# An expert list after the first half of a batch pair, and a routing moved ahead of left-over rounds

## The chip, the cores and the metric

The kernel runs on one core of one Trainium2 chip. The metric is the device time of one execution in microseconds; the median of three runs is shown. Five engines with queues of their own work side by side: PE (matrix multiplication, results go to PSUM), DVE (vector operations), ACT (activation functions and copies), POOL (here mainly indirect DMAs) and SP (DMA issues). Each takes its instructions in the order in which they were written into its queue and waits at the head of the queue for what the instruction needs.

## The reference

Four layers, each added to a running x of 4 sequences of 1024 tokens of width 256, in float32, each behind a layer norm:

```python
# layer 1: gated recurrence over the 1024 tokens, 64 states
m_new = max(m + lf, li); c = exp(m + lf - m_new) * c + exp(li - m_new) * z
x = x + (o * tanh(c)) @ Wp.T + bp
# layer 2: mixture of 8 experts (hidden width 512), the best 2 of each token
p, e = softmax(top_2(xn @ gate.T)); h1, h2 = split(xn @ w12[e].T)
x = x + sum_k p_k * (silu(h1) * h2) @ w3[e].T
# layer 3: causal attention, 16 heads of width 64
# layer 4: mixture of 32 experts (hidden width 128) with the best 4 of each
# token, at most 256 places an expert, and a shared expert beside it
x = x + sum_k w_k * expert[e_k](xn) + shared(xn)
```

## The kernel before

**Order of the work.** Most of the program is written in plain order and a planner sets the order of each engine's queue from it: an instruction that stands earlier in the program goes first when both could run by the planner's own clock, and a later one may fill a gap. Attention's steps (`run_steps`) and PE's part of the first experts (`l2_experts`) are fixed in the order written. The queues are fixed before the program starts[...].

**Layers 1 and 2.** The tokens are cut into four units: unit u is one half (512 tokens) of each of two sequences. `l1_unit(u)` is the recurrence of a unit, `l2_route(u)` its routing. Routing computes the gate scores (L396), takes the best two of eight (L407 to L412), counts how many tokens of each expert stand before each token (L424 to L427), and turns that into a place in a queue of that expert in HBM (`slots`, `row`, L429 to L435). Then POOL writes the rows of x into the queues, 16 indirect DMAs a unit (`scatter`, L245). Each new scatter waits for the eighth before it.

The experts work on tiles of 128 rows of one queue. Which tiles there are is known only at run time, so DVE builds a list on the chip: the lengths of the queues (`l2_lengths`), the whole or part tiles in them (`l2_count`), their running sum (`l2_cum`), an offset for each expert (`l2_shift`), and for each tile its expert and its first row (`l2_tiles`). There are three lists. List A is made after unit 1: 25 tiles (`NQ_A`), the number of whole tiles that 4096 entries in eight queues have at least. Lists B and C are made after unit 3 and hold the rest. `done` says how many tiles of each expert list A has taken. `l2_back` computes for each token in which of the output tiles its two results will lie; for that it adds to the token's place an offset that depends on which list the tile came from, with one bound between each two lists.

`l2_experts` runs over the tiles in the order of the lists. `l2_load` (L578) reads the first row from the list on SP and loads 128 rows; it waits for the last eight scatters of the units that the list covers (`nsent1` scatters for list A, all for B and C). It runs four tiles ahead. A tile is scaled on DVE (L586), transposed (L591), multiplied with the expert's w12 (L608), put through Silu on ACT (L613) and a product on DVE (L614), transposed again (L620, L622), multiplied with w3 (L628), copied (L632) and stored by SP (L633). Until tile 12 the two PSUM results of a tile share one bank; from tile 12 (`T_LATE`), when the recurrence's PSUM banks are free, the output has two banks of its own. The first 68 tiles always run, and three more under a condition.

**Layers 3 and 4.** Attention runs over four sequences, eight pairs of heads each. Beside attention of sequence b+1 runs layer 4's routing of sequence b (`l4_route`, two halves of 512 tokens). Beside the last sequence runs `l4_experts_beside`: twelve expert tiles of the first three sequences, in rounds of two tiles. A round has a load of rows of `xs_d` into `room` on SP and of weights into `w_pairs` on POOL (both in `l4_load`, L1105 and L1110), transposes (`pta`), two matmul steps (`pea`, `pya`), and two indirect DMAs that write the results to `yt_d`. These pieces are a list of jobs (`Beside`), of which attention's steps call a piece here and there. What is left when attention ends is worked off afterwards:

```python
drain(l3_out(B - 1, ps_s, "s"))
while beside.jobs or beside.job is not None:
    beside.step()
late = []
for h in range(2):
    drain(l4_route(B - 1, h, sm, ps_s, "s", late))
```

`l3_out` is attention's output projection (`pz`). All PSUM tiles of these lines come from one pool of seven banks, `ps_s`. `Scatters` is the writer of the routed rows (`to_slots`, into `xs_d`) and of the expert outputs (`to_tokens`, into `yt_d`); its `wait` makes a load wait for the latest eight writes that were issued before it in the program. `l4_route` of the last sequence writes only the first of the four choices at once (eight scatters, L857); the rest stand under a condition.

**The tail.** Behind that come the count of places over the last sequence (`pn`, L1758), the list of its four expert tiles (`l4_list_b`) and a flag on DVE, 24 takes of finished expert outputs of the first three sequences (`l4_take`, L1727, 6.1 MB on SP, which wait for the last eight writes to `yt_d`), a branch on the flag (L1837, L1841), the four expert tiles (`l4_get` and so on, whose row loads wait for the routing's scatters), the adds of all takes (`l4_add`, L1734), eight more takes and the stores of the result.

Of the kernel before, what the change touches and what calls it, by code (L numbers as in the profile page):

```python
# [33 lines left out]


NQ_A = -(-(B * S - E0 * (P - 1)) // P)
NQ_1 = (B * S + E0 * (P - 1)) // P
NQT = (B * S * K0 + E0 * (P - 1)) // P
NQ_S = B * S * K0 // P + E0 // 2
# [17 lines left out]
def block_kernel(  # L57
# [119 lines left out]
    with ExitStack() as ph:  # L177
# [280 lines left out]
        def l2_lengths(u, name):  # L458

            pn = ps_t.tile([P, E0], F32, name=f"pn_{name}", tag="t")  # L460
            nc.tensor.matmul(pn, ones, runs[u][:, NU, :], start=True, stop=True)
            return pn

        def l2_count(pn, op, name):

            n = 2 * NU + 1 if op == ALU.is_le else 4 * NU
            first = 1 if op == ALU.is_le else 0
            more = sm.tile([P, D + 2], F32, name=f"more_{name}", tag="xn", bufs=4)
            more = more[:, : E0 * (n - first)].rearrange("p (e n) -> p e n", e=E0)
            nc.vector.tensor_tensor(  # L470
                more, whole[:, first:n].unsqueeze(1).to_broadcast([P, E0, n - first]),
                pn.unsqueeze(2).to_broadcast([P, E0, n - first]), op,
            )
            cnt = rt.tile([P, E0], F32, name=f"cnt_{name}")
            nc.vector.tensor_reduce(cnt, more, AX.X, ALU.add)
            return cnt

        def l2_cum(cnt, name):
            n = cnt.shape[-1]
            cum = rt.tile([P, n], F32, name=f"cum_{name}")  # L480
            nc.vector.tensor_tensor_scan(cum, ones[:, :n], cnt, 0.0, ALU.mult, ALU.add)
            return cum

        def l2_shift(cum, cnt, start, base, name):

            sh = rt.tile([P, E0], F32, name=f"shift_{name}")
            nc.vector.tensor_sub(sh, cum, cnt)
            if start is not None:
                nc.vector.tensor_sub(sh, sh, start)
            nc.vector.tensor_scalar(sh, sh, float(P), float(P * base), ALU.mult, ALU.add)  # L490
            return sh

        def l2_tiles(cum, shifts, base, skip, n, name):


            ns = len(shifts)
            past = rt.tile([P, n, ns * E0], F32, name=f"past_{name}", tag="past")
            nc.vector.tensor_tensor(
                past, tile_no[:, skip : skip + n].unsqueeze(2).to_broadcast([P, n, ns * E0]),
                cum.unsqueeze(1).to_broadcast([P, n, ns * E0]), ALU.is_ge,  # L500
            )

            val = rt.tile([P, 2, ns * E0 + 1], F32, name=f"val_{name}")
            for s, sh in enumerate(shifts):
                es = slice(s * E0, (s + 1) * E0)
                nc.vector.tensor_copy(val[:, 0, es], expert_no)
                nc.vector.tensor_sub(val[:, 1, es], base1, sh)
            nc.vector.memset(val[:, 0, ns * E0 :], 0.0)
            nc.vector.memset(val[:, 1, ns * E0 :], float(E0 * QROWS + 1))
            step = rt.tile([P, 2, ns * E0], F32, name=f"step_{name}")  # L510
            nc.vector.tensor_sub(step, val[:, :, 1:], val[:, :, : ns * E0])
            out_i = []
            for w in range(2):
                prod = rt.tile([P, n, ns * E0], F32, name=f"prod_{name}_{w}", tag="prod")
                nc.vector.tensor_mul(
                    prod, past, step[:, w, :].unsqueeze(1).to_broadcast([P, n, ns * E0])
                )
                f = rt.tile([P, n], F32, name=f"desc_{name}_{w}")
                nc.vector.tensor_reduce(f, prod, AX.X, ALU.add)
                i = rt.tile([P, n], I32, name=f"desc_i_{name}_{w}")  # L520
                if w == 0:
                    nc.vector.tensor_copy(i, f)
                else:

                    off = rt.tile([P, n], F32, name=f"off_{name}")
                    nc.vector.tensor_scalar(
                        off, past[:, :, ns * E0 - 1], -1.0, float(-P), ALU.add, ALU.mult
                    )
                    pos = rt.tile([P, n], F32, name=f"tile_pos_{name}")
                    nc.vector.tensor_scalar(pos, tile_no[:, skip : skip + n], float(base), None, ALU.add)  # L530
                    nc.vector.tensor_mul(off, off, pos)
                    nc.vector.tensor_add(f, f, off)
                    nc.vector.tensor_scalar(
                        i, f, val[:, 1, 0:1], -1.0, ALU.add, ALU.add
                    )
                out_i.append(i)
            return out_i


        def l2_back(ts, n, shifts, bounds, name):  # L540
            r = sm.tile([P, n, E0], F32, name=f"back_{name}", tag="back", bufs=1)

            def wide(t):
                return t.unsqueeze(1).to_broadcast([P, n, E0])

            first = rt.tile([P, E0], F32, name=f"first_{name}")
            nc.vector.tensor_sub(first, shifts[0], base1)
            nc.vector.tensor_add(r, slots[:, ts, :], wide(first))
            for j, bound in enumerate(bounds):
                lim = rt.tile([P, E0], F32, name=f"lim_{name}_{j}")  # L550
                nc.vector.scalar_tensor_tensor(lim, bound, float(P), base1, ALU.mult, ALU.add)
                dif = rt.tile([P, E0], F32, name=f"dif_{name}_{j}")
                nc.vector.tensor_sub(dif, shifts[j + 1], shifts[j])
                ge = sm.tile([P, n, E0], F32, name=f"ge_{name}_{j}", tag="ge", bufs=1)
                nc.vector.tensor_tensor(ge, slots[:, ts, :], wide(lim), ALU.is_ge)
                nc.vector.tensor_mul(ge, ge, wide(dif))
                nc.vector.tensor_add(r, r, ge)
            back = rt.tile([P, K0, n], F32, name=f"backf_{name}")
            for k in range(K0):
                g = sm.tile([P, n, E0], F32, name=f"bk_{name}_{k}", tag="ge", bufs=1)  # L560
                nc.vector.tensor_tensor(
                    g, slots[:, ts, :], chosen[:, k, ts].unsqueeze(2).to_broadcast([P, n, E0]),
                    ALU.is_equal,
                )
                nc.vector.tensor_mul(g, g, r)
                nc.vector.tensor_reduce(back[:, k, :], g, AX.X, ALU.add)
            back_i = keep0.tile([P, K0, n], I32, name=f"back_{name}")
            nc.vector.tensor_copy(back_i, back)
            return back_i
# [129 lines left out]
        def in_sequence(u):  # L699
            return [(v, n) for par in range(2) for v in (u, u + 1) for n in range(par * HT0, par * HT0 + HT0)]  # L700


        for u in range(2):
            l1_unit(u)
            l2_route(u)
        nsent1 = len(sent)
        pn1 = l2_lengths(1, "half")
        fullA = l2_count(pn1, ALU.is_le, "whole")
        cnt1 = l2_count(pn1, ALU.is_lt, "half")
        cumA = l2_cum(fullA, "whole")  # L710
        shA = l2_shift(cumA, fullA, None, 0, "A")
        listed = [l2_tiles(cumA, [shA], 0, 0, NQ_A, "A")]

        done = rt.tile([P, E0], F32, name="done")
        nc.vector.tensor_sub(done, fullA, cumA)
        nc.vector.tensor_scalar(done, done, float(NQ_A), 0.0, ALU.add, ALU.max)
        nc.vector.tensor_tensor(done, done, fullA, ALU.min)
        seg = rt.tile([P, 2 * E0], F32, name="seg")
        nc.vector.tensor_sub(seg[:, :E0], cnt1, done)
        cumB1 = l2_cum(seg[:, :E0], "B1")  # L720
        shB1 = l2_shift(cumB1, seg[:, :E0], done, NQ_A, "B1")
        back1 = l2_back(slice(0, 2 * NU), 2 * NU, [shA, shB1], [done], "1")


        for u in (2, 3):
# [17 lines left out]
        half = (NQT - NQ_A) // 2  # L743
        listed.append(l2_tiles(cumB, [shB1, shB2], NQ_A, 0, half, "B"))
        listed.append(l2_tiles(cumB, [shB1, shB2], NQ_A, half, NQT - NQ_A - half, "C"))
        back2 = l2_back(slice(2 * NU, 4 * NU), 2 * NU, [shA, shB1, shB2], [done, cnt1], "2")

        first = in_sequence(0)
        adds = {}
# [1 line left out]
        def behind(t):  # L751
# [8 lines left out]

        tiles = [
            (exp_i[0:1, j : j + 1], src_i[0:1, j : j + 1], n)
            for (exp_i, src_i), n in zip(listed, (nsent1, len(sent), len(sent)))
            for j in range(exp_i.shape[-1])
        ]
        with tc.manual_schedule(engines={mybir.EngineType.PE}):
# [492 lines left out]
    def drain(pieces):  # L1259
        for _ in pieces:  # L1260
            pass
# [4 lines left out]
    with ExitStack() as ph:  # L1266
# [430 lines left out]
        with tc.manual_schedule():  # L1697
            run_steps()
        drain(l3_out(B - 1, ps_s, "s"))
        while beside.jobs or beside.job is not None:  # L1700
            beside.step()
        late = []
        for h in range(2):
            drain(l4_route(B - 1, h, sm, ps_s, "s", late))

    taken.close()

# [220 lines left out]
```

## Time and profile before

| what | us |
|---|---|
| median of three runs (2060.64 to 2064.38) | 2062.74 |
| the profiled execution, its own time | 2178.17 |
| its span, first to last instruction | 2176.5 |
| PE busy in it (86%) | 1881.8 |
| DVE busy (58%) | 1258.6 |
| ACT busy (44%) | 959.4 |
| first scatter of units 0, 1, 2, 3 (POOL) | 65.3, 115.2, 178.8, 233.3 |
| first transpose of an expert tile (PE) | 141.2 |
| last matmul of the 68 expert tiles begins | 625.6 |
| attention's output projection ends | about 2074 |

The mean granted clock of PE in the profiled execution is 0.928 of full speed. A line of the page's slices has one digit for each of 40 equal parts of the span (54.4 us each): the busy share of an engine in tenths, or the granted clock in tenths. A line of a timeline has the start in us, the duration in us, the engine, the line of the program, the operation, what it writes and reads, how many instructions were merged, and in brackets how long the engine stood idle before and what ended that. A line of windows has for each stretch the busy time and the number of instructions of PE, PE's weight loads, DVE, ACT and POOL.

### The profile page before, as it was taken

The page shows a single profiled execution, that of the slowest core. Times are in us where ns is not written, and L with a number is a line of the kernel's source. Part 1 is how long each engine was busy: PE and PEld are TensorE (multiplying, and loading weights), DVE is VectorE, ACT ScalarE, POOL GpSimd, SP SyncE. Part 2 cuts the span into 40 slices and gives each one's busy share as a digit, 9 for nine tenths or more (in the row PEclk, how much of TensorE's full clock was granted, in tenths as well). Part 3 has the DMA queues.
Part 4 walks back from the last instruction along what each step waited for, and adds up shares of the span by engine and source line. Part 5 has one row for each costly group of instructions (what it writes and reads, how often), then busy time and mean ns, then how long its engine had stood idle before and what let it go on. Part 6 is the DMA issues. An engine that isn't in the chain of part 4 may idle for free.

```text
span 2176.5 us, 45180 instructions
## 1 busy us (share of the span) xinstructions
PE 1881.8 (86%) x17612; PEld 1223.1 (56%) x17612; DVE 1258.6 (58%) x4101; ACT 959.4 (44%) x2485; POOL 272.3 (13%) x307
## 2 busy tenths in 40 slices
PE   5668799999999999999988979997988997978863
PEld 3434456665656666666555656564655664646642
DVE  5676422234237777656756654774766475757556
ACT  3244222222236666645555543554545363645310
POOL 0333400022003200000020110002020002020121
PEclk7678799999999999999998989998999998989986
DMA  8112211122135433000000000000000000001135
GB/s 328 39 62 68 77 42 48 46 72 77 56 93 165 147 104 116 20 2 2 2 16 6 2 2 1 2 2 1 2 2 2 2 2 2 2 2 57 49 109 183
DMA packets 87151, 109.23 MB, mean 50 GB/s; under 512 B 13838, under 2 KB 76650, under 8 KB 85776
## 3 DMA queue, kind: packets, MB, share of 16 engines
q1 hardware_dynamic: 66528, 73.41, 10.2%
q0 software_dynamic: 15168, 27.05, 4.1%
q10 hardware_dynamic: 5232, 5.78, 0.8%
q8 instruction: 143, 2.34, 0.5%
q14 instruction: 80, 0.66, 0.1%
HBM read 51.75 MB, written 64.77 MB: 54 GB/s over the span
## 4 chain that ended last, share of the span: by engine, by line
PE 49%; DVE 11%; ACT 3%; issue 3%; another core or an unknown queue 3%; DMA 2%; SPq 0%; DVEq 0%; POOL 0%; ACTq 0%; POOLq 0%
PE ps L1450 10%; PE pa L1536 8%; PE pt L1500 7%; PE pq L901 6%; PE pz L901 5%; PE pk L901 5%; PE pv L901 5%; DVE ps L1466 3%; ACT pe L1479 2%; DMA xs_d<-x,row_l 1%; DVE pT L1521 1%; PE s_l L901 1%; DVE nm L1464 1%; PE sy L901 1%
## 5 line engine op out<-in xcount | busy, mean ns | idle before, releaser
L1479 ACT ACTIVATE pe<-ps,nm 128x512 f32<-128x512 f32 (+3 forms) x768 | 439.5, 578 | 279.7 <-DVE nm L1466 268.1
L1536 PE MATMUL pa<-pT,v 128*64 128x128 f32 (+1 forms) x4096 | 326.8, 291 | 3.5 <-issue 3.5
L1500 PE MATMUL pt<-ident,pe 64*128 64x64 f32 x4608 | 251.6, 231 | 90.4 <-ACT pT L1521 34.5
L1500 PEld LDWEIGHTS pt<-ident,pe 64*128 64x128 f32 x4608 | 211.6, 141 | 183.0 <-issue 79.2
L1450 PE MATMUL ps<-k,q 64*128 64x512 f32 (+3 forms) x1536 | 308.1, 509 | 5.5 <-issue 5.5
L1536 PEld LDWEIGHTS pa<-pT,v 128*64 128x64 f32 x4096 | 243.5, 138 | 106.6 <-issue 88.9
L1464 DVE TENSOR_REDUCE nm<-ps 128x1 f32<-128x512 f32 x256 | 175.9, 687 | 147.3 <-PE ps L1450 121.6
L608 PE MATMUL ph<-w_t,xgT 128*128 x544 | 259.2, 618 | 0.7
L1521 ACT COPY pT<-pt 128x512 f32<-128x512 f32 (+2 forms) x384 | 179.4, 520 | 172.6 <-PE pt L1500 163.0
L857 POOL DMA_INDIRECT xs_d<-x,row_l x104 | 102.7, 988 | 1117.6 <-DVE second L1009 1065.4
L1450 PEld LDWEIGHTS ps<-k,q 64*128 64x128 f32 x1536 | 137.7, 191 | 79.7 <-issue 66.9
L1521 DVE COPY pT<-pt 128x256 f32<-128x256 f32 (+3 forms) x384 | 178.5, 506 | 1.8 <-remote 1.5
L1466 DVE CUSTOM_DVE_ANT_0 ps<-ps,mask_a,nm 128x128 f32<-128x128 f32 (+3 forms) x256 | 143.2, 559 | 42.2 <-DVE nm L1464 9.9
L608 PEld LDWEIGHTS ph<-w_t,xgT 128*128 128x128 f32 x544 | 100.9, 197 | 104.5 <-issue 104.4
L1479 ACT ACTIVATION_READ_ACCUMULATOR pe<-ps,nm 128x1 f32 x768 | 152.1, 198 | 0.0
L901 PE MATMUL pq<-l_xT,w_pairs 128*64 128x512 f32 x448 | 110.8, 616 | 29.7 <-ACT pe L1479 28.5
L1466 DVE CUSTOM_DVE_ANT_0 ps<-ps,mask_a 128x128 f32<-128x128 f32 (+3 forms) x256 | 119.7, 518 | 23.5 <-PE ps L1450 21.8
L901 PE MATMUL pz<-wo_t,y 128*64 128x256 f32 x1024 | 115.0, 379 | 0.0
L901 PE MATMUL pv<-w_pairs,l_xT 128*64 128x128 f32 x1792 | 111.3, 278 | 2.9 <-ACT pe L1479 2.9
L628 PE MATMUL py<-w_t,hidT 128*128 x464 | 109.6, 379 | 0.0
L901 PE MATMUL pk<-l_xT,w_pairs 128*64 128x512 f32 x448 | 107.2, 599 | 1.1 <-ACT pe L1479 1.1
L901 PEld LDWEIGHTS pv<-w_pairs,l_xT 128*64 128x64 f32 x1792 | 100.4, 139 | 5.7 <-ACT pe L1479 3.6
(411 smaller groups left out, 2216.0 us busy)
## 6 DMA issues: line engine op xcount, KB each, us to landing
yt_d<-zeros SPq DMA_DIRECT2D x32, 512.0 KB
xg<-xe_d SPq DMA_DIRECT2D x68, 129.0 KB
yq_d<-ys SPq DMA_DIRECT2D x68, 128.0 KB
xs_d<-zeros SPq DMA_DIRECT2D x65, 131.5 KB
w_t<-w_dram SPq DMA_DIRECT2D x8, 1024.0 KB
w_pairs<-e_w_dram POOLq DMA_DIRECT2D x12, 384.0 KB
x<-x_in_dram SPq DMA_DIRECT2D x8, 512.0 KB
w_t<-w_dram SPq DMA_DIRECT2D x8, 512.0 KB
```

Of the source, the lines that this page charges most:

```text
L608: nc.tensor.matmul(pt, xgT[:, c, :], w[:, c, k * H0 : (k + 1) * H0], start=(c == 0), stop=(c == NC_ - 1),)
L628: nc.tensor.matmul(py, hidT[:, c, :], w[:, c, :], start=(c == 0), stop=(c == H0 // P - 1))
L857: i = nc.gpsimd.indirect_dma_start(out=self.out, out_offset=bass.IndirectOffsetOnAxis(ap=idx, axis=0), in_=src, in_offset=None, bounds_che ...
L901: nc.tensor.matmul(out[r], lhsT[:, r], rhs, start=start, stop=stop)
L1450: nc.tensor.matmul(t[:, :n], qs[b, p][rows, i * P : (i + 1) * P], ks[b, p][rows, kc * 512 : kc * 512 + n], start=True, stop=True,)
L1464: nc.vector.tensor_reduce(m[:, 0:1], t, AX.X, ALU.min)
L1466: nc.vector.tensor_tensor_reduce(out=t[:, :n], in0=t[:, :n], in1=mask[:, 512 - n :], scale=1.0, scalar=-LOWEST if kc == 0 else m[:, 0:1], ...
L1479: inst = nc.scalar.activation(pe[:, :n], sps.pop((u, k, par))[:, :n], AF.Exp, bias=ms[u, i, par][:, 1:2], scale=-1.0, accum_out=ls[b, p][: ...
L1500: nc.tensor.transpose(pts[u][r][:, j, par, :], pes[u, k, par][rows, j * P : (j + 1) * P], ident[rows, rows],)
L1521: copy(to, pts[u][r][:, :n])
L1536: nc.tensor.matmul(pas[0][rows, cols], vs[b, p][:, j, rows], pTs[u][:, j, par, a * P :], start=(j == 0), stop=(j == nb - 1),)
```

## The change

In front, unit 0's routing is followed by a list of its own: nine tiles (`NQ_A0`), the number of whole tiles that 2048 entries in eight queues have at least. Their loads wait only for unit 0's scatters. List A after unit 1 then holds the other 16 of the 25, starting behind what the first list has taken; the small helper `l2_listed` computes what a list has taken of each expert, and both calls of `l2_back` get one more offset and one more bound. The number of tiles and their work stay the same. In the tail, the routing of the last sequence is moved in front of the loop that works off the left-over rounds.

```diff
+NQ_A0 = -(-(B * S // 2 - E0 * (P - 1)) // P)
...
-        for u in range(2):
-            l1_unit(u)
-            l2_route(u)
+        def l2_listed(cum, seg, n, name):
+
+            t = rt.tile([P, E0], F32, name=f"among_{name}")
+            nc.vector.tensor_sub(t, seg, cum)
+            nc.vector.tensor_scalar(t, t, float(n), 0.0, ALU.add, ALU.max)
+            nc.vector.tensor_tensor(t, t, seg, ALU.min)
+            return t
+
+
+        l1_unit(0)
+        l2_route(0)
+        nsent0 = len(sent)
+        full0 = l2_count(l2_lengths(0, "unit"), ALU.is_le, "whole0")
+        cum0 = l2_cum(full0, "whole0")
+        sh0 = l2_shift(cum0, full0, None, 0, "A0")
+        listed = [l2_tiles(cum0, [sh0], 0, 0, NQ_A0, "A0")]
+        done0 = l2_listed(cum0, full0, NQ_A0, "A0")
+
+
+        l1_unit(1)
+        l2_route(1)
         nsent1 = len(sent)
         pn1 = l2_lengths(1, "half")
         fullA = l2_count(pn1, ALU.is_le, "whole")
         cnt1 = l2_count(pn1, ALU.is_lt, "half")
-        cumA = l2_cum(fullA, "whole")
-        shA = l2_shift(cumA, fullA, None, 0, "A")
-        listed = [l2_tiles(cumA, [shA], 0, 0, NQ_A, "A")]
-
-        done = rt.tile([P, E0], F32, name="done")
-        nc.vector.tensor_sub(done, fullA, cumA)
-        nc.vector.tensor_scalar(done, done, float(NQ_A), 0.0, ALU.add, ALU.max)
-        nc.vector.tensor_tensor(done, done, fullA, ALU.min)
+        segA = rt.tile([P, E0], F32, name="segA")
+        nc.vector.tensor_sub(segA, fullA, done0)
+        cumA = l2_cum(segA, "whole")
+        shA = l2_shift(cumA, segA, done0, NQ_A0, "A")
+        listed.append(l2_tiles(cumA, [shA], NQ_A0, 0, NQ_A - NQ_A0, "A"))
+        done = l2_listed(cumA, segA, NQ_A - NQ_A0, "A")
+        nc.vector.tensor_add(done, done, done0)
...
-        back1 = l2_back(slice(0, 2 * NU), 2 * NU, [shA, shB1], [done], "1")
+        back1 = l2_back(slice(0, 2 * NU), 2 * NU, [sh0, shA, shB1], [done0, done], "1")
...
-        back2 = l2_back(slice(2 * NU, 4 * NU), 2 * NU, [shA, shB1, shB2], [done, cnt1], "2")
+        back2 = l2_back(slice(2 * NU, 4 * NU), 2 * NU, [sh0, shA, shB1, shB2], [done0, done, cnt1], "2")
...
-            for (exp_i, src_i), n in zip(listed, (nsent1, len(sent), len(sent)))
+            for (exp_i, src_i), n in zip(listed, (nsent0, nsent1, len(sent), len(sent)))
...
         drain(l3_out(B - 1, ps_s, "s"))
-        while beside.jobs or beside.job is not None:
-            beside.step()
         late = []
         for h in range(2):
             drain(l4_route(B - 1, h, sm, ps_s, "s", late))
+        while beside.jobs or beside.job is not None:
+            beside.step()
```

## The prediction

> **What bounds the kernel now.** I read the slices of the span first, then the windows of the first 350 us, then the timelines of each engine at both ends. The slices, then three windows (PE, PEld, DVE, ACT and POOL busy in us, clock, DMA share, GB/s):
>
> ```profile
> PE   5668799999999999999988979997988997978863
> PEclk7678799999999999999998989998999998989986
> 75.00:100.00 25.00, 11.57 (x43) 6.67 (x40) 17.57 (x51) 8.89 (x13) 9.63 (x9) 0.65 0.15 53
> 100.00:125.00 25.00, 14.28 (x55) 10.71 (x54) 17.93 (x126) 6.56 (x11) 7.70 (x8) 0.50 0.10 38
> 300.00:350.00 50.00, 50.00 (x194) 31.38 (x193) 13.16 (x26) 13.19 (x27) 0.00 (x0) 1.00 0.14 43
> ```
>
> From 297 us on PE is full until attention ends near 2074, so whatever PE fails to do before 297 is added to the end one for one. Between 75 and 125 it idles half the time at a clock of 0.50 to 0.65: unit 1 of the first layer and its routing are a chain over PE, DVE and ACT with nothing beside it. The last 100 us are a second such stretch.
>
> **Front: when tiles may start, and how fast they go beside a unit.** On POOL the last scatters of units 0 and 1, on PE the first tile, and the pitch of tiles in steady state:
>
> ```profile
> 85.73 1.33 POOL L245 DMA_INDIRECT xe_d<-x,row  x1 [0.30 <-issue]
> 135.83 0.97 POOL L245 DMA_INDIRECT xe_d<-x,row  x1 [0.30 <-issue]
> 141.20 0.69 PE L591 MATMUL pxy<-ident,xg 128*128 128x128 f32 x2 [6.99 <-DVE l_m L355]
> 277.46 0.44 PE L591 MATMUL pxy<-ident,xg 128*128 128x128 f32 x2 [0.46 <-ACT ys L632]
> 284.28 0.44 PE L591 MATMUL pxy<-ident,xg 128*128 128x128 f32 x2 [0.46 <-ACT ys L632]
> 320.60 0.38 PE L591 MATMUL pxy<-ident,xg 128*128 128x128 f32 x2
> 326.42 0.38 PE L591 MATMUL pxy<-ident,xg 128*128 128x128 f32 x2
> ```
>
> A tile's rows may be loaded when its unit's scatters have landed. The first tile now follows unit 1's last scatter by 141.2 - 136.8 = 4.4 us; behind unit 0's, which ends at 87.06, it stands at about 91.5: 49.7 us earlier. The expert weights have landed by 50 us, so they don't delay it. Beside units 2 and 3, from 141.2 to 231.4, six tiles' hidden matmuls (L608) get through, 15.0 us each. At that rate 49.7 us holds 3.3 tiles, well under the nine offered. They are tiles that now run alone at 6.83 us (277.46 to 284.28; the 5.82 us pitch comes with the second pair of banks at tile 12): 3.3 x 6.83 = 22.6 us saved on PE.
>
> What it costs the units, between their first scatters on POOL (65.32, 115.17, 178.79, 233.28): unit 1 takes 49.9 us with no tile beside it, unit 2 63.6, unit 3 54.5. So tiles lengthen a unit by 54.5 - 49.9 = 4.6. Unit 2's further excess is the A and B lists and the first back list on DVE, and one stop of 5.4 us in which DVE's row scaling (L586) waits for the first tile's rows with unit 2's state update queued behind it. That stop moves to unit 1, where the same rows come first, and leaves unit 2. Unit 1 also gets the new list ahead of it on DVE: some 22 operations of 0.15 to 0.35, about 4 us; the second list loses width and gains five small operations, 0.5. Each back list gains a bound: two operations of 0.16 and three of 0.28, 1.2 us, twice; the first lies between units, the second after unit 3, and I charge 1 in all since PE has tiles there. One matmul of 0.5 is nothing beside this. SP gets nine loads earlier, none more; they lie behind the weight loads, which end at 34.8, and hold nothing up. POOL gets nothing new. Lengthening: 4.6 + 4 + 0.5 + 1 = 10.1, taken against higher clock in unit 1 (the 32 score matmuls, L396, take 7.0 us in unit 1 and 4.25 in unit 3): -2.5, so 7.6. In these 7.6 us another half tile goes through, 3.4. **Front: -22.6 + 7.6 - 3.4 = -18, taken as -17.** Bounds: two tiles and 10 us of lengthening, -4; five tiles and 5 us, -29.
>
> One rule speaks against this. A tile's Silu stands between Tanh, Exp, Sigmoid and Sqrt of the unit; ACT's table loads are 5 in unit 1's 53 us and 9 in unit 2's 63. The row is 1.28 us, and the next activation follows at once (79.40, then 80.70). The Trainium skill ("ScalarE: Activation LUTs", What ACT_TABLE_LOAD costs) gives 1.28 plus a drain, 2.66 us a switch. Four more switches are 5.1 us by the row and 10.6 by the rule, if all lie on the chain; the front would be -17 or -11.5. I hold to the row: units 2 and 3 ran with their switches, and their 4.6 us contains them.
>
> **Tail: the routing goes ahead of four left-over rounds.** PE's timeline (first left-over matmul, last one, first transposes of the two halves of the routing, the count for the last list), then SP's:
>
> ```profile
> 2073.93 1.92 PE L901 MATMUL pea<-room,w_pairs 128*64 128x128 f32 x32
> 2095.12 1.08 PE L901 MATMUL pya<-w_pairs,room 128*64 128x256 f32 x8 [1.49 <-DVE room L1210]
> 2096.14 1.09 PE L929 MATMUL pt_l<-ident,xn_l 128*128 128x128 f32 x8
> 2109.59 1.09 PE L929 MATMUL pt_l<-ident,xn_l 128*128 128x128 f32 x8
> 2128.17 0.38 PE L1758 MATMUL pn<-run_l,ones 128*128 128x32 f32 x2 [1.28 <-DVE sh_l L1026]
> 2110.76 17.26 SPq L1727 DMA_DIRECT2D yg<-yt_d  x24
> 2140.36 2.86 SPq L1110 DMA_DIRECT2D xg<-xs_d  x4
> ```
>
> The rounds take 2073.93 to 2096.1, 22.2 us; the routing then 32. Exchanged, the routing starts 22.2 earlier: its normalized rows were ready at 2067. But I read here that both draw their PSUM tiles from one ring in program order. The second half's transposes wait until 2109.59, behind the first half's shared matmuls, though its rows are ready at 2098.3 and PE idles 4.7 us meanwhile; pn, of the next stage, waits for the routing's last reader (L1026). So the rounds will not fill the routing's gaps; they start when its last shared matmul is issued, and pn waits for their last tile. From L947 to L1001 DVE needs 10.8 us in the routing's second half and 9.1 in the first, since adds of the takes stand in between; those will come later, so the routing shrinks from 32 to some 30 us and its last s_l matmul ends at 2104. Rounds: 22.2, at the row.
>
> A new wait: the rounds' four room loads on SP (L1110) wait for the latest eight scatters into xs_d, now those of this routing. The last of these come some 6 us after the row numbers, and the second round stops for about 2.5. Behind those loads on SP stand only the takes, late anyhow. Their w_pairs loads and eight scatters on POOL pass behind the routing's eight scatters, which now meet an idle POOL. Last round's end: 2104 + 22.2 + 2.5 = 2128.7; pn 2129.4, against 2128.2. **The 22 us are given back**: list and flag come at about 2134.5, as now.
>
> What becomes late next: the 24 takes (L1727), 6.1 MB, 17.26 us on SP, wait for the last left-over scatter to land, now at 2100.8. After the change: 2128.7 + 0.6 (copy) + 2.6 (two scatters) + 1.3 = 2133. They run to 2150.5. If they keep their place in front of the flag's load, the branch and the last four xg loads in SP's queue, xg goes at 2150.5 + 3 = 2153.5 instead of 2140.4, 13 us late. From xg on the present 36 us follow, less about 3 since the 24 adds of 0.4 us that DVE mixes in there now lie mostly earlier. Tail +10. If the branch goes first, xg stands at 2140, the takes run 2143 to 2160, and the last eight takes (now 2161.9) are hardly moved: 0. Both are ready within 2 us; the takes stand first in the program, so I take +10. Bounds: if my ring is wrong and rounds fill the gaps, the whole lead, -20; +16 if the routing keeps its 32 us and the rounds lose 4.
>
> The Trainium skill ("TensorE: Matmul & The Clock Gate", Part 1) halves PE's clock after about 3.4 us of idling. The routing has two longer gaps on PE, so the rounds could start cold: pea was 1.95 warm, 3.19 at 2090.44. By the rule four rounds lose some 2.1 us each, 8 in all; by the row, three of four ran warm with gaps under 2 us and none or one is slow. I take none and keep 4 in the bound above.
>
> **Sum.** On the profiled execution: 2178.17 (span 2176.5 and 1.7 around it) - 17 + 10 = 2171. That execution is 115 us above the median of the runs; the chain shows two blank stretches of 17 us in it, and the front and the tail are no part of these. I carry the difference over unscaled: 2062.74 - 7 = **2055.7, say 2055.5**. No change means within 0.2%, 4.1 us, the spread of the three runs.
>
> **Rivals.** (a) As above, 0.43; own range 2047 to 2065. (b) The tail costs nothing or gains, since the branch overtakes the takes or rounds fill gaps: 2062.7 - 17 - 0 to 10, about 2043. For it: the takes and the flag are ready 2 us apart. Against: the ring. 0.26. (c) The tiles are ready but find no room, two get through: -4 and the tail +5, 2063; DVE is busy 70% of these 50 us, but PE has 24 us free there. 0.12. (d) Slower: PE takes instructions in written order, and tiles written among unit 1's matmuls hold its chain. At 172.15 four ph matmuls (3.78 us) stand between unit 2's two slot matmuls. Four tiles, each holding the chain for its whole path from ph to ys, 8.5 us, lengthen unit 1 by 34: +8 in front, +10 in the tail, 2080. With the tail at +10 it is slower from a lengthening of 22 us, 5.5 a tile; unit 3 showed 1.5 a tile. 0.19, which takes in a tail past its bound. That the move does nothing in front is excluded by the free PE.
>
> Range: (b) down to 2037 and (d) up to about 2073 leave out 2 in 10. Faster: most of (b), two thirds of (a), 0.54. Same: a fifth of (a), half of (c), 0.18. Slower: (d) and the rest, 0.28.
>
> **What would show it.** In front: first L591 near 92 us; nine or ten tiles by 231 instead of six; the clock in 100 to 125 above 0.6; unit 1 between first scatters at about 60 us; last py near 610 instead of 629. In the tail: first pt_l near 2074 less the front's gain, pea only after the last s_l, pn waiting for the copy of pya, the takes in one block ahead of xg. It is wrong if pea stands between pt_l and s_l, if xg precedes the takes, or if units 1 to 3 take over 185 us.

## The result and the profile after

The changed kernel takes 2067.28 us (median of 20 runs, 2063.76 to 2075.69), the kernel before on the same chip 2062.56 (20 runs): a ratio of 1.0029, with a 95% interval of 1.0019 to 1.0039. It is **4.7 us slower**. The forecast was 7 us faster.

The profiled execution of the changed kernel is from this chip: it took 2066.96 us, its span is 2065.0. The experiments below ran on two other chips; there the kernel before takes 2174 to 2178 us. By its time of 2178 us the profile of before came from such a chip too, though that is not on record. So the two spans must not be subtracted. I cut each profile into three parts instead: up to attention's first `pq`, attention to the end of `pz`, and the tail behind it. A second profile of before (`b_copy`) and one of the changed kernel (`a_copy`), both from the slower chip, stand beside them.

| us | first tile | first pq | attention | tail | pn, from pz's end | takes, duration | xg, from pz's end |
|---|---|---|---|---|---|---|---|
| before | 141.2 | 630.1 | 1444.0 | 102.4 | 54.1 | 17.26 | 66.3 |
| b_copy | 140.2 | 623.0 | 1446.7 | 101.6 | 53.8 | 17.12 | 66.1 |
| after (faster chip) | 90.0 | 599.5 | 1348.6 | 116.8 | 52.4 | 24.48 | 84.5 |
| a_copy | 90.7 | 610.6 | 1443.8 | 122.0 | 56.6 | 24.39 | 88.7 |

The difference between the chips is nearly all in attention (95 us), which the change doesn't touch. The front became shorter, the tail longer.

**Front.** POOL's timeline of the changed kernel (first and last scatter of unit 0, first of unit 1), then PE's (first tile), then two windows (PE, PE's weight loads, DVE, ACT and POOL busy, clock, DMA share, GB/s):

```profile
64.33 1.22 POOL L246 DMA_INDIRECT xe_d<-x,row  x1 [60.43 <-DVE row L436]
...
84.64 0.97 POOL L246 DMA_INDIRECT xe_d<-x,row  x1 [0.30 <-issue]
121.89 1.06 POOL L246 DMA_INDIRECT xe_d<-x,row  x1 [36.28 <-DVE row L436]
```

```profile
89.96 0.69 PE L592 MATMUL pxy<-ident,xg 128*128 128x128 f32 x2 [8.32 <-DVE l_last L366]
```

```profile
75.00:100.00 25.00, 14.07 (x50) 7.26 (x47) 15.33 (x33) 7.28 (x9) 8.44 (x8) 0.72 0.27 85
100.00:125.00 25.00, 23.46 (x103) 13.88 (x101) 21.08 (x138) 13.61 (x22) 2.50 (x3) 0.94 0.08 24
```

The first tile stands 4.3 us behind the end of unit 0's last scatter on POOL (84.64 + 0.97 to 89.96), 51 us earlier than before. Between 100 and 125 us PE is busy for 23.5 us of 25 where it was busy for 14.3, and its clock is 0.94 where it was 0.50. Unit 1 takes 57.6 us between first scatters instead of 49.9.

**Tail.** PE's timeline (the routing's first transposes, its last shared matmuls, then the left-over rounds and the count for the last list), then SP's:

```profile
1948.10 1.09 PE L946 MATMUL pt_l<-ident,xn_l 128*128 128x128 f32 x8
...
1972.48 3.69 PE L918 MATMUL s_l<-xT_l,sw_t 128*64 128x512 f32 x13
...
1975.60 2.31 PE L918 MATMUL pea<-room,w_pairs 128*64 128x128 f32 x32
...
1998.04 1.08 PE L918 MATMUL pya<-w_pairs,room 128*64 128x256 f32 x8 [1.48 <-DVE room L1227]
...
2000.53 0.41 PE L1775 MATMUL pn<-run_l,ones 128*128 128x32 f32 x2 [1.41 <-ACT room L1210]
```

```profile
1981.62 5.43 SPq L1127 DMA_DIRECT2D room<-xs_d  x4
2004.49 24.48 SPq L1744 DMA_DIRECT2D yg<-yt_d  x24
2032.69 3.47 SPq L1127 DMA_DIRECT2D xg<-xs_d  x4
2050.61 4.89 SPq L1744 DMA_DIRECT2D yg<-yt_d  x8
```

The order is the one forecast: routing, then all rounds, then `pn`, which waits for the copy of the last `pya` (PE idles 1.41 us until ACT's L1210 is done). The 24 takes stand in one block ahead of `xg`. But the block lasts 24.48 us, not 17.26. The DMA view of these two stretches says why. Before, from 2110.76 to 2128.02 (first line the total, then queue, packets, MB, share):

```profile
DMA packets 3151, 5.87 MB, mean 340 GB/s; under 512 B 502, under 2 KB 2126, under 8 KB 3150
...
q1 hardware_dynamic: 2958, 5.84, 92.6%
q0 software_dynamic: 192, 0.02, 0.9%
```

After, from 2004.49 to 2028.97, with the issues of the two queues that are new in it:

```profile
DMA packets 4520, 8.41 MB, mean 344 GB/s; under 512 B 411, under 2 KB 2983, under 8 KB 4519
...
q1 hardware_dynamic: 2887, 5.78, 70.3%
q0 software_dynamic: 576, 1.57, 17.9%
q10 hardware_dynamic: 1056, 1.05, 12.4%
...
ew<-e_w_dram POOLq DMA_DIRECT2D x4, 384.0 KB, 8.9
out_dram<-x ACTq DMA_DIRECT2D x2, 512.0 KB, 7.5
```

The rate is the same, 340 and 344 GB/s, and the DMA engines are busy for shares of 0.94 and 1.01 of these stretches (the windows below): they are full both times. Before, the takes had them to themselves. After, the weights of the last four experts (1.57 MB) and two stores (1.05 MB) go at the same time: 2.62 MB at 344 GB/s are 7.6 us, and the block is 7.2 us longer. What else runs in these stretches:

```profile
2110.76:2128.02 17.26, 7.50 (x56) 4.83 (x56) 14.52 (x65) 1.53 (x4) 3.84 (x5) 0.70 0.94 340
```

```profile
2004.49:2028.97 24.48, 0.00 (x0) 0.00 (x0) 17.29 (x44) 0.00 (x0) 2.19 (x4) 0.50 1.01 344
```

In the kernel before (first) PE and ACT work on the routing's second half while the takes run. In the changed kernel (second) PE and ACT stand still for the whole of it; DVE adds what has arrived.

### The profile page after: what moved, and what is told of

It is laid out like the page before. It is cut to its first block, busy times and chain, and to the rows that moved or that the text cites. A ratio compares the mean times of both kernels' runs of the same rounds, so it can differ in the third digit from the quotient of the medians.

```text
span 2065.0 us, 45229 instructions
## 1 busy us (share of the span) xinstructions
PE 1844.5 (89%) x17614; PEld 1207.5 (58%) x17614; DVE 1264.2 (61%) x4138; ACT 960.3 (47%) x2487; POOL 274.4 (13%) x307
## 3 DMA queue, kind: packets, MB, share of 16 engines
q1 hardware_dynamic: 66528, 73.41, 10.8%
## 5 line engine op out<-in xcount | busy, mean ns | idle before, releaser
L1467 PE MATMUL ps<-k,q 64*128 64x512 f32 (+3 forms) x1536 | 297.5, 504 | 0.0
L1517 PEld LDWEIGHTS pt<-ident,pe 64*128 64x128 f32 x4608 | 207.7, 141 | 114.3 <-issue 54.1
L1517 PE MATMUL pt<-ident,pe 64*128 64x64 f32 x4608 | 242.0, 231 | 28.3 <-ACT pe L1496 27.9
```

The source lines that it names most:

```text
L1467: nc.tensor.matmul(t[:, :n], qs[b, p][rows, i * P : (i + 1) * P], ks[b, p][rows, kc * 512 : kc * 512 + n], start=True, stop=True,)
L1517: nc.tensor.transpose(pts[u][r][:, j, par, :], pes[u, k, par][rows, j * P : (j + 1) * P], ident[rows, rows],)
```

## The experiments

My theory at this point (theory 1): the front is as forecast, the lead of the routing is given back through the ring of PSUM tiles, and the takes in SP's queue make the tail longer. All experiments ran on the slower chips; each ratio is against the kernel before on the same chip.

**The kernel before once more**, unchanged, to see which of its marks move from one execution to the next.

> The kernel before once more, for a second profile of it. The first profiled execution of it took 2178 us against 2062 of its timed runs, and its trace shows blank stretches; the profile of the changed kernel took 2067, as its runs do. Theory (the first profile was disturbed): this one takes about 2062, its expert tiles end 20 to 25 us later than in the changed kernel (595 us), not 30, and attention takes the same time in both. Rival (attention itself became faster or slower by the change): the stretch from the last expert matmul to the end of attention's output projection differs between the two by more than 5 us.

Measured: 2172.97 us beside a median of 2177.66. Its first `pq` stands 7 us earlier than in the first profile, its attention is 2.7 us longer, its tail 0.8 shorter. So a single profile fixes the front only to some 7 us, and the 2178 us of the first profile were no disturbed execution but this chip's usual time.

**The front alone.**

```diff
+        while beside.jobs or beside.job is not None:
+            beside.step()
         late = []
         for h in range(2):
             drain(l4_route(B - 1, h, sm, ps_s, "s", late))
-        while beside.jobs or beside.job is not None:
-            beside.step()
```

> The changed kernel with the tail as it was before: the list of nine tiles alone. Theory (front and tail are separate, the front gains and the tail takes it back): the changed kernel is 4.7 us above the kernel before, and its trace shows 116.9 us from the end of attention's projection to the end against 102.5 before, 14.4 more; so this one should be 4.7 - 14.4 = 9.7 us below the kernel before, near 2053. Rival (the front gains nothing): 2062. Rival (the front gains its 17 to 30 us in full and the middle loses): 2040 or below, or 2062 with a longer attention.

Measured: 2165.74 us, 0.9939 (0.9918 to 0.9961), 13.3 us faster (8.5 to 17.9). SP's timeline of the tail is as before, with 17.44 us of takes:

```profile
2096.12 17.44 SPq L1744 DMA_DIRECT2D yg<-yt_d  x24
2125.67 2.87 SPq L1127 DMA_DIRECT2D xg<-xs_d  x4
```

The first `pq` is at 608.9 us. Over all nine profiles with this front from the slower chips it is at 609.5 in the mean, against 627.5 over the three with the old front: 18 us.

**The tail alone**: the kernel before, with the last two hunks of the change.

```diff
-        while beside.jobs or beside.job is not None:
-            beside.step()
         late = []
         for h in range(2):
             drain(l4_route(B - 1, h, sm, ps_s, "s", late))
+        while beside.jobs or beside.job is not None:
+            beside.step()
```

> The kernel before with the routing of the last sequence ahead of the left-over rounds, and the front as it was. Theory: 14 us slower than the kernel before, about 2077, with the rounds' first matmul behind the routing's last shared matmul on PE and the 24 takes in one block ahead of the last four row loads on SP. Rival (the tail costs nothing and the front loses 5): 2062.

Measured: 2200.66 us, 1.0105 (1.0082 to 1.0127), 23 us slower. The tail is 122.1 us instead of 102, `pn` at 57.0 as late as before, the takes last 26.81 us and `xg` goes at 91.0 instead of 66.

**The rounds with a PSUM bank of their own**: the changed kernel, but the rounds behind attention draw from the bank of the weighted sums.

```diff
+        class RoundsPS:
+            own = False
+            def tile(self, shape, dt, name, tag):
+                if self.own:
+                    return ps_a.tile(shape, dt, name=name, tag="a")
+                return ps_s.tile(shape, dt, name=name, tag=tag)
+        rounds_ps = RoundsPS()
...
-                                sm, ps_s, "s", lambda j: w_pairs[:, j],
+                                sm, rounds_ps, "s", lambda j: w_pairs[:, j],
...
             drain(l4_route(B - 1, h, sm, ps_s, "s", late))
+        rounds_ps.own = True
         while beside.jobs or beside.job is not None:
```

> The changed kernel, with one difference: the left-over rounds take their PSUM tiles from attention's one-bank pool of weighted sums, which is idle by then, instead of from the seven banks that the routing draws on. Theory (the rounds can't fill the routing's gaps because both draw tiles from one ring in program order, and pn waits for the ring's last reader): the rounds' matmuls now stand between the routing's, pn comes right behind the routing's last shared matmul, and the rounds end some 5 to 10 us earlier; since the takes then start earlier by as much, the end comes 5 to 10 us earlier than in the changed kernel, 2057 to 2062. Rival (the rounds wait for something else, such as their rows or POOL): same order on the chip and same time, 2067.

Measured: 2183.09 us, 1.0022 (1.0012 to 1.0032). The ring is confirmed: with another bank the first `pea` comes 0.95 us behind `pz` instead of 27 to 31, and `pn` at 29.6 instead of 52 to 57. Yet `xg` stays at 89.2 and the tail at 121.3. The later rounds still wait on SP for the routing's scatters, the takes for the rounds' last scatter, and the takes (24.26 us) stand ahead of `xg`. The wait that I had named for `pn` was real, and removing it was worth nothing.

**The changed kernel on the slower chip.**

> The changed kernel as it is, beside the others on one chip. If the two halves add up (0.9939 for the front alone, 1.0105 for the tail alone), 1.004 of the kernel before, with the tail from the end of pz at 117 to 122 us. If the chip makes the difference, anything from 1.001 to 1.007.

Measured: 2177.47 us, 0.9996 (0.998 to 1.0011). The tail is 122.0 us, 20 longer than before. The two halves measured alone give 0.9939 x 1.0105 = 1.0043, outside this interval. The medians alone (2177.47 against 2174.08) give 1.0016; single runs spread over 1% on this chip, and what makes the difference stays open.

**The takes behind `xg` in the queue.** The list of takes is issued only once the loads of the four expert tiles have been.

```diff
-        ygs = [l4_take(*u) for u in known]
+        ygs = []
...
             loads = [l4_get(j0 + k, k, lst) for k in range(n)]
+            if j0 == 0:
+                ygs.extend(l4_take(*u) for u in known)
```

> The changed kernel with one edit: the 24 takes of left-over rows are issued on SP behind the loads of the last four expert tiles. Theory 1 (the tail's loss is the takes' 24 us standing ahead of xg on SP): xg goes some 12 us after pn, near 65 us behind pz's end instead of 84.5; the takes then run to about 91 and the last eight behind them, the tail ends at 104 to 107 instead of 117, the whole 10 to 13 us faster than the changed kernel and some 6 to 8 faster than the kernel before. Rival (the loss is the bytes, not the order): takes and their adds end last wherever they stand, and the tail stays at 114 or more.

Measured: 2169.61 us, 0.9967 (0.9949 to 0.9984): 7 us faster than before, 8 than the changed kernel beside it. SP's timeline:

```profile
2110.10 0.33 SPq L1744 DMA_DIRECT2D yg<-yt_d  x1
2111.86 2.86 SPq L1127 DMA_DIRECT2D xg<-xs_d  x4
2114.81 38.32 SPq L1744 DMA_DIRECT2D yg<-yt_d  x31
```

`xg` goes at 62.6 us, 26 earlier than in `a_copy`, earlier even than I had written. The tail falls only to 113.7. The other 31 takes now fill SP to the end, and POOL's scatters of the four tiles begin at 2143.2, 16 us behind the last row copy on ACT (2126.98). The order in the queue gives back less than half of what was lost. POOL's row and a window (PE, PE's weight loads, DVE, ACT and POOL busy, clock, DMA share, GB/s):

```profile
2143.23 1.04 POOL L874 DMA_INDIRECT yt_d<-ys,to_i_b  x1 [27.47 <-DMA out_dram<-x]
2133.00:2136.00 3.00, 0.00 (x0) 0.00 (x0) 3.00 (x9) 0.00 (x0) 0.00 (x0) 0.92 0.10 30
```

The tail is as long as the rival had it, but its reason, the bytes, isn't shown by it. What ended the scatters' wait is a DMA that landed, not a row copy; in SP's waits the takes themselves stop for 4.9 us for a store of the result (`out_dram`) to land (until 2135.25), and in the second half of that stop the DMA engines move 30 GB/s. So a part of what remains are waits that this order brought along: in the program the takes, which read `yt_d`, now stand between `xg` and these scatters, which write it. Whether that is the reason, and how long the tail would be without these waits, no run shows.

**Both edits together.**

```diff
+        rounds_ps.own = True
...
-        ygs = [l4_take(*u) for u in known]
+        ygs = []
...
+            if j0 == 0:
+                ygs.extend(l4_take(*u) for u in known)
```

> The same edit, and the rounds behind attention also draw their PSUM tiles from the bank of the weighted sums. Theory 1: pn comes near 30 us behind pz's end as it did with the bank alone (which gained nothing, since the takes behind the rounds' last scatter still stood ahead of xg), and now xg can go once the rounds' last room loads have left SP, near 50. The takes start near 61 as the rounds' last scatter lands, and end last: tail 96 to 101 us, 15 to 20 us faster than the changed kernel. Rival (PE, DVE and POOL have no room for routing, rounds and expert tiles side by side): within 4 us of the kernel with the takes moved alone.

Measured: 2168.01 us, 0.9973 (0.996 to 0.9985); no better than the takes alone. The tail of the profile is 120.9 us, in an execution of 2177.39 us, the slowest of 22. `pn` stands at 31.6, but `xg` only at 68.6. DVE's timeline shows that the list, of which the count had been there for 28 us, begins when the last round's `pya` is done:

```profile
2115.47 0.43 DVE L1092 TENSOR_TENSOR eql<-key_b,entry 128x256 f32<-128x256 f32 x1 [2.16 <-PE pya L918]
```

`eql` is a tile of the next stage's pool. I think that it lies in the memory of the rounds' weights, which that `pya` reads; no run tried another place for it. The scatters of the four tiles stop here too, for 27.65 us, until a store has landed. So of theory 1 the ring and the place in the queue are real but not what decides, and a second theory took its place (theory 2): **the takes cost nothing before because the routing's second half ran beside them; behind the rounds nothing of that length is left to run beside them, so their transfer is paid, wherever it stands in the queue.**

**All but one take left out**, with the changed tail and with the old one. One take is loaded, and all adds read it: the adds are as many, and 23 of the 24 transfers are left out.

```diff
-        ygs = [l4_take(*u) for u in known]
+        one = l4_take(*known[0])
+        ygs = [one for _ in known]
```

The changed kernel with it:

> The changed kernel with 23 of the 24 takes left out: one is loaded, and all 24 adds read it (left-over rows are wrong, the adds on DVE are as many). Theory 2 (the takes' transfer of 6 MB lay beside the last routing and was hidden; behind the rounds nothing lies beside it, so wherever it stands in the queue it is paid): xg goes 12 us behind pn, near 68 us behind pz's end instead of 89, and the tail falls from 122 to 100 to 103. Rival (the rounds are slower behind the routing, by clock and by room loads that wait for its scatters): the tail stays at 110 or more.

The front alone with it:

> The front half of the change alone, tail order as before, with the same 23 takes left out. Theory 2: they were hidden here, so the tail stays within 3 us of its 102, and this kernel and the one above, which differ in the order of the tail alone, lie within 0.002 of each other, where with the takes they lie some 0.006 to 0.010 apart. Rival: this one is 10 us or more faster than the one above.

Measured: 0.9936 (0.9917 to 0.9956) and 0.9927 (0.9914 to 0.994). Without the takes the order of routing and rounds makes no difference beyond the intervals. The tails are 105.9 and 104.1 us, where with the takes they are 122.0 and 102.2. SP's timelines, the changed kernel first:

```profile
2107.23 0.33 SPq L1744 DMA_DIRECT2D yg<-yt_d  x1
2114.74 2.85 SPq L1127 DMA_DIRECT2D xg<-xs_d  x4
2132.99 4.41 SPq L1744 DMA_DIRECT2D yg<-yt_d  x8
```

```profile
2089.14 0.33 SPq L1744 DMA_DIRECT2D yg<-yt_d  x1
2118.91 2.85 SPq L1127 DMA_DIRECT2D xg<-xs_d  x4
2139.95 5.55 SPq L1744 DMA_DIRECT2D yg<-yt_d  x8
```

`pz` ends at 2047.2 in the first (by the first `pt_l` at 2047.13) and at 2050.4 in the second, so `xg` goes at 67.5 and 68.5: equally late. The takes cost 16 us in the changed order and nothing in the old one. Both tails end 2 to 4 us above the 102 of before; the next kernel's, with the old order and all takes, is 105.5, so this much may be scatter between executions. The pair shows that the whole cost of the new order hangs on these transfers. Whether they cost by their bytes or by their place ahead of `xg`, it doesn't separate; and since the kernel with the takes behind `xg` has waits of its own, the words "wherever it stands in the queue" stay unproven.

**Four tiles instead of nine** behind the first unit, with the old tail.

```diff
-NQ_A0 = -(-(B * S // 2 - E0 * (P - 1)) // P)
+NQ_A0 = 4
```

> The front half of the change alone (tail as before), with four tiles behind the first unit's routing instead of nine. If only some three tiles get through before the second list is there (as the traces show: 3 done by 178 us in place of 1), four are as good as nine: 0.9939 within 0.0015, 13 us faster than before. Rival (the longer list itself feeds the tiles beside unit 2): a gain of 6 us or less.

Measured: 2165.91 us, 0.9954 (0.9936 to 0.9972), 10 us faster than before. That is between the two expectations: the interval takes in the 13 of nine tiles and ends at the 6 of the rival. Two tiles have ended their w3 matmuls by 178 us (nine: 3; before: none or 1), 13 by 300 (nine: 14 to 16; before: 11 or 12). Most of the gain comes from the first four, as three tiles' worth would have it; whether the rest is real isn't settled.

**Routing and rounds side by side, in the old order.** If the takes are to stay covered, the rounds have to stay ahead of the routing's end. So: the front alone, and the last routing draws its PSUM tiles from the bank of the weighted sums.

```diff
-            drain(l4_route(B - 1, h, sm, ps_s, "s", late))
+            drain(l4_route(B - 1, h, sm, ps_a, "a", late))
```

> The front half alone, with the last routing's PSUM tiles drawn from the bank of the weighted sums, so that routing and left-over rounds, in their old order, can run side by side. Theory 2: the routing starts with pz's end instead of 22 us behind it, the rounds keep their place and so do the takes, which lie beside the routing as before; pn near 45 us behind pz's end instead of 54, xg near 58 instead of 66, tail 94 to 97: 0.990, some 20 us faster than the kernel before. Rival (the one bank makes the routing slow, or the list waits for the rounds' buffers as with the bank for the rounds): tail 101 or more, no better than the front alone (0.994).

Measured: 2152.24 us, 0.9897 (0.988 to 0.9914), **22 us faster than before** and the fastest of all. PE's timeline (first round, first and second half of the routing, the count) and SP's:

```profile
2053.15 1.92 PE L918 MATMUL pea<-room,w_pairs 128*64 128x128 f32 x32
...
2055.49 0.60 PE L946 MATMUL pt_l<-ident,xn_l 128*128 128x128 f32 x4
...
2083.11 0.66 PE L946 MATMUL pt_l<-ident,xn_l 128*128 128x128 f32 x4 [0.79 <-DVE sh_l L1043]
...
2094.51 0.64 PE L1775 MATMUL pn<-run_l,ones 128*128 128x32 f32 x2
```

```profile
2085.18 17.29 SPq L1744 DMA_DIRECT2D yg<-yt_d  x24
2116.14 2.87 SPq L1127 DMA_DIRECT2D xg<-xs_d  x4
2136.36 4.96 SPq L1744 DMA_DIRECT2D yg<-yt_d  x8
```

`pz` ends at 2053.3. The routing starts 2 us behind it instead of 22, `pn` comes at 41.2 instead of 54, and the takes run their 17.29 us beside the routing's second half. `xg` goes at 62.8, the tail is 97.1. Of the 13 us that `pn` gains the tail keeps 5: from `pn` to `xg` it is 21.6 us here instead of 12, and ahead of `xg` the chain that ended last has the landing of an expert weight load, from 2108.49 for 7.30 us. So this tail has a next wait already.

**The same from the other side**: the rounds in the old order, but in the bank of their own (with the class `RoundsPS` of above).

```diff
+        rounds_ps.own = True
+        while beside.jobs or beside.job is not None:
+            beside.step()
         late = []
         for h in range(2):
             drain(l4_route(B - 1, h, sm, ps_s, "s", late))
-        while beside.jobs or beside.job is not None:
-            beside.step()
```

> The same aim by the other side: the rounds behind attention draw from the bank of the weighted sums, the routing stays in the ring, and the rounds stay first in the program. Theory 2: the routing needs its 32 us and pn comes near 35, but the rounds, one bank for all their tiles, take 8 to 10 us each instead of 5.5 and end near 35, so the takes run from 38 to 56 and xg goes near 60: tail 96 to 99. Rival: the rounds lose so much that the takes end up behind everything again, tail 105 or more.

Measured: 2162.75 us, 0.995 (0.9937 to 0.9963); the tail is 103.9 us, between the two expectations. With one bank the rounds stretch, the takes start at 42.9 instead of 36.5 and last 25.64 us, since `pn`, at 43.9, brings the expert weights into the same stretch again (8.49 MB at 331 GB/s).

## Why the prediction was wrong

- **Front, -17: right in its mechanism; the size is shown on the slower chips alone.** First tile forecast near 92 us, measured 90.0; the clock in 100 to 125 above 0.6, 0.94; unit 1 about 60 us, 56.7 to 61.0; units 1 to 3 not over 185, 165 to 171; last `py` near 610, 598 on the faster chip and 604 to 611 on the slower ones. Nine or ten tiles by 231 were forecast in place of six: by their hidden matmuls 9.0 to 9.9, and 6 to 7 before, so some 2.6 more where 3.3 were taken. The lengthening was put at 7.6 over the three units: unit 1 took 8 to 13 more, units 2 and 3 some 3 less each, and the sum is 168.7 in the mean of six profiles against 164.6 in three of before, 4 us. The two misses nearly cancel. By the first `pq` the gain is 18 us, by the run times 13.3 (8.5 to 17.9). That each us of the front counts one for one at the end, since PE is full until 2074, is therefore not shown: PE's slices in the prediction have 7 to 9 tenths from about 1090 us on.
- **Head of line on PE (the slower rival): no.** Its sign was right, its mechanism wasn't: no unit was held by 22 us.
- **ACT's table loads:** two more in the three units, not four (23 before, 25 after), so row and rule part by only 2.8 us, which the run times can't tell. The trace of before speaks for the row: around 15 of its table loads the next activation starts 1.30 to 1.33 us behind the end of the last one, which leaves no room for a drain.
- **The 22 us are given back through the ring: right**, as the order of `s_l`, `pea`, `pya` and `pn` shows and the bank of its own confirms. But it was not what decides: with the ring out of the way the tail was as long.
- **Cold rounds:** of the 8 us by the rule on the clock gate (the Trainium skill, "TensorE: Matmul & The Clock Gate", Part 1: half speed after some 3.4 us of idling), of which I took none, little was paid. In the first profile after, PE's stops between the rounds are 1.4 to 2.35 us, and the four `pea` took 2.31, 1.95, 2.64 and 1.94. On the slower chip one stop ahead of a `pya` is 3.39 us, and the `pea` behind it took 3.66; that agrees with the rule, and is some of the 4 us by which its takes start later (60.6 against 56.3). But it took no such stop in the first profile: the third `pea` (2.64) and the `pya` ahead of it (1.98 instead of 1.08, at a granted clock of 0.50) stand behind stops of 2.35 and 1.49 us with four transposes between them.
- **The step that failed: "the 24 takes (L1727), 6.1 MB, 17.26 us on SP", carried to a new place at the duration of the old one.** The start was forecast at 58.9 us behind `pz`'s end and is at 56.3; from the end of the takes to `xg` I had 3.0 and there were 3.7; the relief behind `xg` was 3 and is 3.8. The block itself is 24.48 us. In its new place it falls together with the experts' weights and the first stores, which wait for the same point in time, and the DMA engines were full already. With 24.5 in the sum the tail is +17 instead of +10 and the total 0 instead of -7. Measured: +14.4 on the faster chip, against the tail of before from the slower one, and +20 on the slower ones. The total was +4.7, so on the faster chip the front would have given about 10 us (4.7 - 14.4) and not 17; with no profile of before from that chip this is an estimate, and where the other 7 are stays open.
- **Behind it a wrong question.** I asked where the takes stand in the queue, and named as the favourable rival that `xg` goes first, for 0. With `xg` first 113.7 of the 122.0 remain, in part through waits of that order. What had to be asked was what covers the transfer: before, the routing's second half did, and with 23 takes left out the two orders come within 2 us of each other.
- **The base.** I read the 115 us between profile and median as part of a disturbed execution. By the runs on record it is most likely another chip. The number was carried unscaled either way, and the front and tail marks, apart from the takes, differ little between the chips, so this cost nothing here.

## What to carry to other kernels

A transfer that is hidden has its price all the same; when work is moved, list which work covered which transfer and put every moved transfer beside its new neighbours at the rate of full DMA engines, bytes over rate, not at the duration that it had alone. Taking a wait away (a ring, a place in a queue) shows little as long as a second one, ready at nearly the same time, stands behind it, or the new order brings waits of its own; leaving the transfer out showed what it costs where two runs with other orders could not. And look for the overlap that changes no order: giving the routing another bank kept the cover of the takes and gained 22 us with the front.

## What was not expected of the hardware

One and the same kernel takes 2062.6 us on one chip and 2174 to 2178 on two others, with the mean granted clock at 0.949 on the first (changed kernel) and 0.929 on another. In the changed kernel the front differs by some 10 us between the chips and the tail by 5; the rest lies in attention, 1348.6 us against 1438 to 1451. On the slower chips PE stands still for 11 to 13 us at three places of attention, each beside the 16 scatters behind a routing's second half (until 1264, 1639 and 1933 us of the kernel before), and ACT and DVE wait for an event that the profile only calls remote. On the faster chip no such stop is to be seen beside the same scatters. They make up 34 of the 95 us (10.8, 10.9 and 12.2 in the kernel before); what causes them, and the rest of the 95, stays open.
